# Two transformer blocks on one core: the first mixture slot's rows and weights loaded beside the last attention cells, the tile search cut into steps, one norm moved ahead

## The chip, the core and the metric

The kernel runs on one core of a Trainium2 chip. The core has a matrix engine (PE, with its weight loads shown as PEld), a vector engine (DVE), a scalar engine (ACT), a general engine (POOL), and a queue engine (SP) that issues most transfers. Each engine works through its own list of instructions in order and waits on semaphores where it needs another's result. The metric is the device time of one launch in microseconds.

## The reference

The input `x` is two batches of 1024 tokens of width 256. Two blocks follow each other. All arithmetic is in float32.

- Block 0: self attention with 16 heads of width 16, cross attention to a context of 64 rows, and a mixture of experts: every token is normed, a router picks the 2 best of 8 experts, and the token gets the gated sum of two feed-forward results (256 to 1024, gelu, back to 256), added to `x`.
- Block 1: self attention, cross attention with a mask on the context, and one dense feed-forward of the same size. Each step is preceded by a layer norm and added to `x`.

```
x = latents + mha(ln(latents));  x = x + mha(ln(x), ln(tokens))
logits = ln(x) @ rw.T;  vals, idx = top_k(logits, 2);  gates = softmax(vals)
x = x + sum_k gates[k] * (gelu(ln(x) @ fc1[idx_k].T) @ fc2[idx_k].T)
```

## The kernel before

**Cells and tasks.** Self attention of a block is cut into 128 cells, each with the scores of one head for 128 keys and 512 queries. `self_attention` walks over the cells and, between them, lets a `Stream` of tasks emit other work: projections, cross attention, routing. A task is a Python generator. A positive yield is the cost of what it has emitted; a yield of zero or below asks for a pause before its next step. While cells run, any such pause lasts at least one cell (2.9 us in the planner's count). After the last cell, `Stream.rest` emits what is left: it always takes the able task of the highest rank, and keeps a planner's clock that tells it when a paused task may go on. The order that comes out is fixed when the kernel is built: an instruction that stands behind another on its engine waits for it, whatever the planner thought.

**Units.** The tokens are handled in four units of 512 (0 to 3). For each unit, after its self attention: `project` adds the attention result to `x_sb` (L426 products, L434 addition); `cross_tasks` adds three tasks, a norm (`cnorm`), `weigh` (scores, softmax weights, product) and `share`; `dispatch_task` norms the unit again, routes it (L1268 router product, L1278 to L1357 the choice of two experts and the places) and scatters its rows to `sorted_rows` in memory with eight indirect transfers from POOL (L1365). Then `Mixture.find` works out, from counts so far, which expert each tile of 256 sorted rows belongs to (`expert_tiles` L1378 to L1391, `Places.make` L1413 to L1468, a chain of small DVE instructions) and `Mixture.rows` allows the loads of those rows.

**Slots.** A slot is one tile of 256 rows of one expert. `load_rows` fetches its rows (`xs`), `load_weights` its expert's weights in two halves (`w0` of 2056 columns and `w1` of 2304), each by two transfers on SP. The expert's number and the row come from tables in SBUF that SP reads first (L1495). `turn` transposes the rows (L1550 on PE), applies the norm's scale (L365 on ACT) and works out targets and gates (L1556 to L1573, seven small DVE instructions). `first` makes the hidden layer (L1584 on PE, gelu L1590 on ACT), `second` the result (L1614 on PE, L1607 and L1623 on DVE, an indirect store L1629 on POOL). The first slot has what it needs once units 0 and 1 are dispatched; slots 1 to 4 need unit 2, the others unit 3.

In the kernel before, all tiles for slots lie in pools (`slotw`, `epool`) that open only after the last cell, in memory that the attention used. So the first slot's rows and weights start after it. In `rest`, the task of finding (rank 65) and the routing (70) stand above the norm of unit 3's cross attention (40), and the parts of `find` follow each other without a pause there, since its pauses are only made while cells run:

```
            if maxima[0]:
                yield 0.0
```

`maxima[0]` is true while score cells still need their maxima. `weigh` has two forms by the same switch: with cells running, DVE takes maxima and POOL subtracts; after them, DVE does both (L1101, L1102). The order in the second form is a list of steps: `SC` scores of two row groups (L1081), `TU` transposes of them (L1117) and the exponential on ACT (L1121), `PR` the product with the values and the sums (L1130, L1140) with a reciprocal on DVE (L1149), `DI` the division (L1155 on PE, L1162 on DVE).

**Around the change.** The last heads end with `finish`: sums and results are sent to memory (L470, L471), gathered (L475), the inverse of the sums (L486 on DVE) is sent (L487 `turns`), read back spread out (L491 `by_s`) and multiplied in (L497 on DVE); only then can `project` of unit 3 go on PE (L426).

Of the kernel before, what the change touches and what calls it, by code (L numbers as in the profile page):

```python
# [50 lines left out]
P = 128  # L51
# [148 lines left out]
def two_blocks(  # L200
# [814 lines left out]
    def cross_tasks(stream, layer, n, pool, first):  # L1015


        att = 2 * layer + 1
        w = weights[att]
        b, t0 = n // 2, 4 * n  # L1020
        name = f"c{layer}{n}"
        held = {}

        def norm():
            xT = held["xT"] = pool.tile([P, 2, 512], F32, tag="cx", name=f"xT_{name}")
            yield from norm_task(t0, 4, "cq" if layer == 0 else "ln1", xT, name)
            if layer == 0:
                add_bias(t0, 4, bias_out[1])

        before = [(m, n - 1) for m in ("cross", "weighed")] if n > 0 else ["context"]  # L1030
        stream.add(norm(), 2.0, mark=("cnorm", n), after=before[1:], first=first,
            rank=40)
        stream.add(
            weigh(layer, b, pool, w, name, held), 17.0,
            mark=("weighed", n), after=[("cnorm", n), before[0]], rank=30,
        )
        stream.add(
            share(w, name, t0, held), 5.0, mark=("cross", n),
            after=[("weighed", n)], rank=50,
        )  # L1040

    def weigh(layer, b, pool, w, name, held):
# [148 lines left out]
        for step, *args, wait in (  # L1191
            (SC, 0, 0, None),
            (SC, 0, 1, -1.0),
            (TU, 0, 0, None),
            (SC, 1, 0, None),
            (TU, 0, 1, None),
            (SC, 1, 1, None),
            (PR, 0, None),
            (TU, 1, 0, None),
            (DI, 0, None),  # L1200
            (TU, 1, 1, -1.6),
            (PR, 1, None),
        ):
            step(*args)
            yield {SC: cost, TU: 1.15, PR: 1.1, DI: 0.55}[step]
            if wait:
                yield wait
# [190 lines left out]
    class Places:  # L1398
# [3 lines left out]
        def make(self, pool, name, n, had, caps, last):  # L1402
# [14 lines left out]
            nc.vector.tensor_copy(end[:, E:], caps[-1])  # L1417
            if maxima[0]:
                yield 0.0
            upto = pool.tile([P, 2 * E], F32, tag="ntu", name=f"ntu_{name}", bufs=1)  # L1420
# [9 lines left out]
            self.who = const.tile([P, n], F32, name=f"who_{name}")  # L1430
            if maxima[0]:
                yield 0.0
            row = pool.tile([P, n], F32, tag="row", name=f"row_{name}", bufs=1)
# [5 lines left out]
            nc.vector.tensor_copy(self.at[:, 0, :], row)  # L1439
            if maxima[0]:  # L1440
                yield 0.0

            nc.vector.tensor_tensor(over, over, end.unsqueeze(1).to_broadcast(shape), ALU.mult)
            nc.vector.tensor_reduce(row, over, AX.X, ALU.add)
            nc.vector.tensor_tensor(row, number, row, ALU.subtract)
            if maxima[0]:
                yield 0.0
            nc.vector.tensor_scalar(row, row, begin[:, 0:1], 256.0, ALU.add, ALU.mult)
# [3 lines left out]
            nc.vector.tensor_copy(self.at[:, 1, :], row)  # L1452
            if maxima[0]:
                yield 0.0
            if last:
# [14 lines left out]
    class Mixture:  # L1470
# [3 lines left out]
        def __init__(self, slotw, epool):  # L1474
# [3 lines left out]
            self.caps = []  # L1478


            self.w, self.done, self.ready = ({}, {}), [0, 0], (set(), set())
# [21 lines left out]
        def load_rows(self, s):  # L1503
            xs = self.epool[0].tile([P, 2, WIDE], F32, tag="xs", name=f"xs_{s}", bufs=3)
            row = self.number(s, 1, NROWS - 256)
            nc.sync.dma_start(
                out=xs, in_=sorted_rows[bass.ds(row, 256), :].rearrange("(c p) n -> p c n", p=P)
            )
            self.xs[s] = xs

        def load_weights(self, s, half):
            n = NFF - W_2 if half else W_2
            w = self.w[half][s] = self.slotw[0].tile([P, n], F32, tag=f"w{half}", name=f"w{half}_slot{s}")
            e = self.number(s, 0, E - 1)
# [5 lines left out]
        def load(self, most=NSLOT):  # L1520


            if not self.slotw:
                return
            while len(self.xs) < min(self.nrows, self.turned + 3, self.end):
# [3 lines left out]
            for s in range(min(known, most)):  # L1529
                for half in range(2):  # L1530
                    if s == len(self.w[half]) and s < self.done[half] + 2:
                        self.load_weights(s, half)
# [107 lines left out]
        def find(self, units):  # L1640
# [8 lines left out]
            else:  # L1649

                caps = [self.caps[last], *expert_tiles(f"{units}", (ANY if last else FULL,))]
            if maxima[0]:
                yield 0.0
            pool = self.epool[1] if self.epool else const
# [125 lines left out]
    def block(layer, tail, heads=None, beside=None):  # L1780
# [48 lines left out]
        def when_ready(b, qh, stream, cell):  # L1829
            n = 2 * b + qh  # L1830
            cross_tasks(stream, layer, n, pools["cpool"], cell + 1)
            if layer == 0:
# [7 lines left out]
                if n == 1:  # L1840
                    stream.add(
                        mixture.find(2), 0.3, mark=("found", 2), after=[("counted", 1)], rank=65
                    )
            elif n < 2:
                stream.add(
# [25 lines left out]
    for n in range(2):  # L1871
        epool.append(
            slots.enter_context(tc.tile_pool(name=f"epool{n}", bufs=2 - n, side="right"))
        )
    for units in range(2, 5):
        if units > 2:
# [3 lines left out]
            )  # L1880
        stream.add(
            mixture.rows(units), 0.0, mark=("rows", units), rank=75,
            after=[("found", units), ("dispatch", units - 1)],
        )
    for s in range(NFULL[-1]):
# [181 lines left out]
```

## Time and profile before

| | us |
|---|---|
| median of 3 runs (lowest, highest) | 1640.39 (1638.42, 1646.78) |
| the profiled execution | 1651.84 |
| its span, first to last instruction | 1650.1 |
| PE busy | 1591.0 (96%) |
| DVE, ACT, POOL busy | 981.7, 911.6, 415.2 |
| mean granted PE clock | 0.974 |

The page of the profile gives busy times, the span in 40 slices, and the chain of work that ended last. The trace behind it can be asked for stretches of time, for waits, and for single instructions; the times below are microseconds from the start of the span. A float32 matmul is recorded as two instructions, so a count of 16 in the trace is 8 matmuls in the code.

### The profile page before, as it was taken

Reading aid. Unit: us, or ns where it says so; the run is one execution under the profiler, and the core shown is the slowest. Engines: PE = TensorE matmul, PEld = TensorE weight load, DVE = VectorE, ACT = ScalarE, POOL = GpSimd, SP = SyncE. Lnnn points to the kernel's source line nnn. Section 1 sums busy time; section 2 is a strip of 40 time slices with the busy share of each in tenths; the row PEclk is TensorE's granted clock in tenths of the full one; section 3 lists DMA queues with packets and bytes.
Section 4 is the critical chain, followed back from the end, with each engine's and each line's share of the span. In section 5 each row is a group of like instructions: output and inputs, shape, how many; then the busy total and the mean of one; then the engine's idle time right before and its main releaser. Section 6 shows DMA issues by size and latency. Waiting matters only on the chain.

```text
span 1650.1 us, 28271 instructions
## 1 busy us (share of the span) xinstructions
PE 1591.0 (96%) x10682; PEld 878.9 (53%) x10682; DVE 981.7 (59%) x2092; ACT 911.6 (55%) x1768; POOL 415.2 (25%) x549
## 2 busy tenths in 40 slices
PE   7999999999999977999999999999999999999998
PEld 3433344444443435778888763344444435546766
DVE  5687857688678636431113466876767777845400
ACT  2277867667666853324322327876776676673321
POOL 2134324234335202040112122411322323321000
PEclk7799999999999988999999999999999999999999
DMA  4333510110000024256556421000110002000000
GB/s 141 123 130 113 183 31 21 28 33 31 30 21 34 27 81 167 87 202 237 189 188 236 145 65 34 21 27 14 40 37 23 21 14 82 15 14 21 14 13 26
DMA packets 56591, 122.09 MB, mean 74 GB/s; under 512 B 12546, under 2 KB 26756, under 8 KB 56068
## 3 DMA queue, kind: packets, MB, share of 16 engines
q1 hardware_dynamic: 52612, 110.08, 20.6%
q0 software_dynamic: 3456, 9.51, 1.6%
q8 instruction: 86, 1.41, 0.4%
q10 hardware_dynamic: 384, 0.66, 0.2%
q14 instruction: 53, 0.43, 0.1%
HBM read 72.14 MB, written 39.42 MB: 68 GB/s over the span
## 4 chain that ended last, share of the span: by engine, by line
PE 88%; DVE 7%; DMA 2%; issue 2%; ACT 1%; another core or an unknown queue 0%; POOL 0%; SPq 0%; DVEq 0%; POOLq 0%; ACTq 0%
PE banks L758 16%; PE banks L747 15%; PE banks L809 14%; PE banks L1584 8%; PE banks L1614 8%; PE banks L624 4%; PE banks L1757 3%; PE banks L426 3%; PE banks L1745 3%; DVE mx_s L754 2%; PE banks L594 2%; PE banks L1051 2%; PE banks L1117 2%; PE banks L1081 2%; PE banks L358 1%
## 5 line engine op out<-in xcount | busy, mean ns | idle before, releaser
L754 DVE TENSOR_REDUCE mx_s<-banks 128x1 f32<-128x512 f32 x1024 | 634.5, 683 | 208.9 <-PE banks L747 205.0
L764 ACT ACTIVATE pt_s<-banks 128x512 f32<-128x512 f32 x1024 | 531.2, 607 | 149.6 <-PE banks L747 125.6
L747 PE MATMUL banks<-KS,QS 16*128 16x512 f32 x2048 | 537.2, 638 | 4.2 <-issue 1.9
L758 PE MATMUL banks<-qb_s,KS 32*128 32x512 f32 x2048 | 506.8, 617 | 8.0 <-DVE qb_s L704 4.2
L822 POOL TENSOR_TENSOR acc_s<-acc_s,part_s 128x512 f32<-128x512 f32 x143 | 181.9, 1272 | 429.3 <-ACT part_s L821 417.1
L758 PEld LDWEIGHTS banks<-qb_s,KS 32*128 32x128 f32 x2048 | 176.2, 184 | 179.9 <-DVE mx_s L754 105.4
L809 PE MATMUL banks<-pt_s,v_s 128*20 128x512 f32 x2048 | 262.3, 605 | 0.3 <-ACT pt_s L764 0.2
L747 PEld LDWEIGHTS banks<-KS,QS 16*128 16x128 f32 x2048 | 199.2, 188 | 77.8 <-issue 36.0
L1590 ACT ACTIVATE h_s<-banks,w_slot 128x256 f32<-128x256 f32 x160 | 67.1, 471 | 175.9 <-issue 88.8
L1614 PE MATMUL banks<-w_slot,h_s 128*128 128x256 f32 x640 | 145.0, 383 | 2.8 <-ACT h_s L1590 2.8
L1584 PE MATMUL banks<-xsT,w_slot 128*128 128x256 f32 x640 | 147.0, 382 | 0.7 <-ACT xsT L365 0.7
L809 PEld LDWEIGHTS banks<-pt_s,v_s 128*20 128x20 f32 x2048 | 42.8, 98 | 181.3 <-ACT pt_s L764 128.8
L1614 PEld LDWEIGHTS banks<-w_slot,h_s 128*128 128x128 f32 x640 | 121.8, 192 | 23.5 <-ACT h_s L1590 3.2
L1584 PEld LDWEIGHTS banks<-xsT,w_slot 128*128 128x128 f32 x640 | 119.7, 191 | 20.8 <-DVE mx_s L754 2.3
L821 ACT COPY part_s<-banks 128x512 f32<-128x512 f32 x157 | 93.8, 597 | 63.9 <-PE banks L809 54.8
L1623 DVE SCALAR_TENSOR_TENSOR ys<-banks,gate,b 128x256 f32<-128x256 f32 x40 | 19.3, 483 | 170.3 <-PE banks L1614 166.6
L1629 POOL DMA_INDIRECT results<-ys,to x40 | 38.8, 970 | 268.1 <-DVE ys L1623 224.4
L624 PE MATMUL banks<-xT_s,w_att 128*128 128x512 f32 x128 | 68.1, 667 | 0.0
L1748 ACT ACTIVATE h_f<-banks,w_ff 128x512 f32<-128x512 f32 x32 | 22.0, 688 | 75.0 <-PE banks L1745 75.0
L1102 POOL TENSOR_TENSOR sc_c<-sc_c,mx_c 128x512 f32<-128x512 f32 x38 | 39.6, 1044 | 77.9 <-DVE mx_c L1101 77.9
L1757 PE MATMUL banks<-w_ff,h_f 128*128 128x256 f32 x256 | 57.3, 380 | 0.0
L1745 PE MATMUL banks<-hT_f,w_ff 128*128 128x512 f32 x128 | 56.3, 593 | 0.0
(257 smaller groups left out, 1503.4 us busy)
## 6 DMA issues: line engine op xcount, KB each, us to landing
w_slot<-in_ff_w_dram SPq DMA_DIRECT2D x40, 576.0 KB
w_slot<-in_ff_w_dram SPq DMA_DIRECT2D x40, 514.0 KB
sorted_rows<-fill SPq DMA_DIRECT2D x36, 520.0 KB
whole<-acc_s SPq DMA_DIRECT2D x32, 256.0 KB
xs<-sorted_rows SPq DMA_DIRECT2D x20, 260.0 KB
ot_s<-whole SPq DMA_DIRECT2D x16, 256.0 KB
by_s<-turns SPq DMA_DIRECT2D x16, 256.0 KB
y<-results SPq DMA_DIRECT2D x16, 256.0 KB
```

The source lines that it names most:

```text
L624: nc.tensor.matmul(p, lhsT=w[:, at + k * D + pair * P : at + k * D + (pair + 1) * P], rhs=xT[b][:, k, blk * 512 : (blk + 1) * 512], start= ...
L747: nc.tensor.matmul(sc, lhsT=QS[h % 4][r, qc * P : (qc + 1) * P], rhs=K[r, kh * 512 : (kh + 1) * 512], start=True, stop=True,)
L754: return i, lambda: nc.vector.tensor_reduce(mx[h][:, qc, j, kh : kh + 1], sc, AX.X, ALU.max)
L758: nc.tensor.matmul(sc, lhsT=K[r, n * P : (n + 1) * P], rhs=QB[h][r, :], start=True, stop=True)
L764: nc.scalar.activation(pt, sc, AF.Exp, scale=SCALE)
L809: nc.tensor.matmul(o[32 * j : 32 * j + VW, :], lhsT=V[b][:, cell % 8, 4 * g + j, :], rhs=exps.pop((cell, j)), start=(cell == cells[0]), st ...
L821: nc.scalar.copy(part, o)
L822: helper().tensor_tensor(acc[h], acc[h], part, ALU.add)
L1584: nc.tensor.matmul(ph[:, n, :], lhsT=w[:, at : at + P], rhs=xT[:, k, :], start=(k == 0), stop=(k == 1),)
L1614: nc.tensor.matmul(py, lhsT=h1[:, f, h * P : (h + 1) * P], rhs=w[:, f * D : (f + 1) * D], start=(f == 0), stop=(f == 7),)
L1745: nc.tensor.matmul(ph, lhsT=w1[:, at : at + P], rhs=hT[:, k, :], start=(k == 0), stop=(k == 1))
L1757: nc.tensor.matmul(py[:, n, :], lhsT=h1[:, f, t * P : (t + 1) * P], rhs=w2[:, f * D : (f + 1) * D], start=(f == 0), stop=(f == 7),)
```

## The change

- Slot 0's rows get a tile of their own (`xs_0`) and every third slot's first half of the weights another (`spare`), both in the pool that exists from the start. `load` brings slot 0's two while cells still run, as soon as unit 1 is dispatched and searched; the task `rows` of unit 2 moves into the block for that. The first half of the weights may now be three slots ahead, not two.
- `load` is called once more when the pools open, which emits the second half of slot 0's weights there.
- All pauses in `find` and `make` become `-0.9` and are always made.
- The norm of a unit's cross attention gets rank 67 in block 0, above the search (65).
- In the second form of `weigh`, `PR 0` comes before `SC 1 1`, and `TU 0 1` gets a pause of 1.3.

```diff
-            rank=40)
+            rank=67 if layer == 0 else 40)
...
-            (TU, 0, 1, None),
+            (TU, 0, 1, -1.3),
+            (PR, 0, None),
             (SC, 1, 1, None),
-            (PR, 0, None),
...
-            if maxima[0]:
-                yield 0.0
+            yield -0.9
...
+            self.spare = const.tile([P, W_2], F32, name="spare")
...
-            xs = self.epool[0].tile([P, 2, WIDE], F32, tag="xs", name=f"xs_{s}", bufs=3)
+            if s == 0:
+                xs = const.tile([P, 2, WIDE], F32, name="xs_0")
+            else:
+                xs = self.epool[0].tile([P, 2, WIDE], F32, tag="xs", name=f"xs_{s}", bufs=3)
...
-            w = self.w[half][s] = self.slotw[0].tile([P, n], F32, tag=f"w{half}", name=f"w{half}_slot{s}")
+            if half == 0 and s % 3 == 0:
+                w = self.spare
+            else:
+                w = self.slotw[0].tile([P, n], F32, tag=f"w{half}", name=f"w{half}_slot{s}")
+            self.w[half][s] = w
...
             if not self.slotw:
+                if self.nrows and not self.xs:
+                    self.load_rows(0)
+                    self.load_weights(0, 0)
                 return
...
-                    if s == len(self.w[half]) and s < self.done[half] + 2:
+                    if s == len(self.w[half]) and s < self.done[half] + 3 - half:
...
                         mixture.find(2), 0.3, mark=("found", 2), after=[("counted", 1)], rank=65
                     )
+                    stream.add(
+                        mixture.rows(2), 0.0, mark=("rows", 2), rank=75,
+                        after=[("found", 2), ("dispatch", 1)],
+                    )
...
+    mixture.load()
     for units in range(2, 5):
         if units > 2:
...
-        stream.add(
-            mixture.rows(units), 0.0, mark=("rows", units), rank=75,
-            after=[("found", units), ("dispatch", units - 1)],
-        )
+            stream.add(
+                mixture.rows(units), 0.0, mark=("rows", units), rank=75,
+                after=[("found", units), ("dispatch", units - 1)],
+            )
```

The pause in the third piece of the diff stands six times in the change, five of them in `Places.make` and one in `Mixture.find`. As built, the changed kernel has the same number of instructions on every engine; only their order differs. On PE, after the last attention product, the old order is: transposes of the routing norm (8), transposes of slot 0 (4), router product (2), transposes of the logits (4), `first` of slot 0 (8), projection (8, with the two counting products L1328, L1329 between), `first` (8), counting L1378, `second` (16). The new order is: transposes of slot 0 (4), of the routing norm (8), `first` (4), router product (2), `first` (4), transposes of the logits (4), `first` (8), projection (8, with the same two between), counting, `second` (16). On DVE, the norm of unit 3 now stands in front of most of `find`, whose rest is spread between the norm's last steps. On SP, slot 0's rows and first half stand ahead of head 14's send, its second half ahead of head 15's send, and nothing stands between head 15's gather and its `turns`.

## The prediction

> **What bounds the kernel now.** First the page. PE is busy nearly all the time, and two parts of it hold most of the rest.
>
> ```profile
> PE 1591.0 (96%) x10682; PEld 878.9 (53%) x10682; DVE 981.7 (59%) x2092; ACT 911.6 (55%) x1768; POOL 415.2 (25%) x549
> PEclk7799999999999988999999999999999999999999
> PE 88%; DVE 7%; DMA 2%; issue 2%; ACT 1%; another core or an unknown queue 0%; POOL 0%; SPq 0%; DVEq 0%; POOLq 0%; ACTq 0%
> ```
>
> The chain that ended last is PE for 88%: time is won only where PE stands idle or runs at a lowered clock. The start (first two digits of the clock row) isn't touched. The second dip, near 620 us, is where the change works. The waits of PE from 560 to 760 us:
>
> ```profile
> PE banks L358 <- DVE xd_m L1255: 5.9, 1, 5.9
> PE banks L358 <- DVE xn_c L346: 5.3, 2, 4.1
> PE banks L1550 <- DMA xs<-sorted_rows: 3.0, 1, 3.0
> PE banks L1155 <- DVE inv_c L1149: 2.9, 1, 2.9
> PE banks L1614 <- ACT h_s L1590: 2.8, 1, 2.8
> PE banks L1117 <- DVE sc_c L1102: 1.6, 3, 0.8
> ```
>
> Columns: total us, times, longest. The first three are the routing norm of unit 2, the norm of unit 3 and slot 0's rows. Then stretches of the clock (PE busy is the second number, the granted clock the third from the right):
>
> ```profile
> 597.70:601.10 3.40, 0.00 (x0) 0.00 (x0) 2.70 (x16) 0.00 (x0) 0.00 (x0) 1.00 0.21 80
> 601.10:604.50 3.40, 1.97 (x8) 1.54 (x8) 1.64 (x5) 1.72 (x4) 0.00 (x0) 0.50 0.66 174
> 607.90:611.30 3.40, 3.27 (x4) 0.27 (x2) 0.00 (x0) 0.96 (x3) 0.00 (x0) 0.50 0.81 315
> 631.80:635.20 3.40, 0.81 (x4) 0.38 (x2) 1.65 (x10) 0.00 (x0) 1.36 (x2) 1.00 0.94 301
> 642.00:645.40 3.40, 3.40 (x6) 1.34 (x5) 0.00 (x0) 0.69 (x1) 0.00 (x0) 0.50 1.01 401
> 659.10:662.50 3.40, 0.74 (x6) 0.75 (x7) 2.57 (x4) 0.49 (x1) 0.00 (x0) 1.00 0.00 0
> 662.50:665.90 3.40, 3.40 (x15) 3.18 (x14) 0.69 (x1) 1.52 (x3) 0.00 (x0) 0.50 0.00 0
> ```
>
> After a stretch with little work the clock is half; it returns only after a full one. So idle costs twice: the router product, from the PE timeline, at half and at full clock:
>
> ```profile
> 607.59 3.58 PE L1268 MATMUL banks<-hT_m,rw 128*8 128x512 f32 x4
> 689.95 1.88 PE L1268 MATMUL banks<-hT_m,rw 128*8 128x512 f32 x4
> ```
>
> Last the queue. SP issues slot 0's weights ahead of the inverse sums, whose transfer then takes 7.8 us:
>
> ```profile
> 602.56 2.26 SPq L1518 DMA_DIRECT2D w_slot<-in_ff_w_dram  x4
> 604.92 0.55 SPq L487 DMA_DIRECT2D turns<-sums_s  x1
> 612.75 0.69 SPq L491 DMA_DIRECT2D by_s<-turns  x1
> ```
>
> At the head pair before (550.94) the same `turns` needed 1.5 us, and `by_s` after it 3.6.
>
> **Part 1: rows and weights early.** The table for unit 2 is ready at 551.2 and unit 1's last scatter is issued at 532.0, so SP can issue the early loads between 553 and the next send at 570.4; the 1.3 MB land long before 595.7, where the last attention product ends. No transfer waits behind them until 570.4, and PE is covered by cells there: cost nothing. If SP were held to 580, head 14's send has until 597.
>
> From 595.7 on PE, old: idle to 601.62 (5.9), transposes 1.97, idle 3.0, slot 0's transposes, router product 3.58, and so on; counting L1378 starts at 625.32. New, with durations of the trace:
> - Slot 0's transposes at 595.7 (0.60 at full clock). The wait for `xd_m` stays: the DVE list up to L1255 is unchanged (601.16). Idle 5.3 instead of 5.9, so the clock still falls.
> - 601.6: transposes 2.0 at half clock; from here PE has work without a break. The return of the clock needs a full stretch of 3.4, begun at an unknown phase: between 605.0 and 608.4, I take 606.7. `first` (4 matmuls, 1.86 full) crosses it: to 607.0. Router product 1.88: 608.9. `first` 1.86 hides the ACT step lT (0.68, old wait 0.77): 610.7. Logits 0.4: 611.1. `first` 3.6: 614.7.
> - Projection needs `by_s`. Slot 0's second half (1.18 MB) now waits on SP for the last L809 (595.7), stands ahead of head 15's send, and takes 3.5 us at 340 GB/s (rows of 601 to 611). That send is issued at 597.1 as before but lands about 602 (before 599.8). L486 now stands behind seven small DVE instructions: 604.2. `turns` 604.3, lands 606.2; `by_s` 609.8. L497 follows L1281 at 611.4 and ends 612.1: no wait before 614.7, 2.6 us to spare. If that cover went, each us late delays projection and routing by one.
> - The routing choice on DVE (612.1, some 13 instructions of 0.22) gives `chosen` at 614.8, needed at 616.5. Projection 3.6 and counting products 0.7: 619.0; L1378 ends 619.2 against 625.6. **PE is 6.2 us ahead.**
>
> **Part 2: norm before search.** `second` of slot 0 (7.15) ends at 626.4. Second L434 ends at 619.8 (before 622.76). Behind it stood 3.3 of statistics and places, 5.1 of search (26 instructions, 625.89 to 631.0), 4.35 of the root chain, b 0.6, ys. Now: statistics 3.3, three search instructions 0.6, b 0.6, root chain 2.9 to 4.4 (14 of 0.2; old stalls 1.5 may stay), five search 0.8, ys 0.4, four search 0.8: first `xn_c` at 629.2 to 630.6, transposes 0.4 later, 629.6 to 631.0 against 636.67: 5.7 to 7.1 ahead. The PE wait stays 3 to 4.6 (was 4.1). The second pair comes 2.9 behind the first (eight search instructions and a ys between), before 2.4: minus 0.5. What the moved search delays: slot 1's weights issue at 631 to 632.4 (before 629.65), its rows two transfers later at about 635.5 (before 638.88, behind twice the weights), landed about 641. PE's slot 1 and 2 transposes ask for them about 642, in front of the cross attention's transposes.
>
> **The clock there.** The Trainium skill, "TensorE: Matmul & The Clock Gate", Part 1, lets the clock fall after a window of 3.4 us that was idle. Taken strictly, a pause of about 3.9 holds a whole idle window rarely (0.5 of 3.4), and L1051 would run 4 matmuls in about 3.8 (twice L1268's 1.88) instead of 5.99: 2.2 more gained, 3.4 with the transposes. But here the clock fell after 659.1 to 662.5, which was 22% busy with a pause of only 2.85. I go by the row: half clock again, L1051 5.99, nothing gained. Ahead after L1051: **6.0** (5.2 to 6.6).
>
> **Part 3: order in `weigh`.** Counting from L1081's start (646.73 old): DVE takes 1.33 per row group. Old: six groups, 14 turn instructions 2.2, two groups, then L1149 at 660.75; PE waited 0.8, 0.3, 0.6, 2.85, and then 3.4 us ran at half clock (1.6 lost). L426 ended at 32.05. New, from TU 0 1 (ends 7.3): four `first` 1.9, PR 0 1.9, SC 1 1 1.1, TU 1 0 (its scores ready at 11.4) to 13.5; L1149 already at 11.4 to 12.35, so DI 0 13.5 to 14.5 without wait; TU 1 1 to 15.8 (last group 15.0); `first` 17.7, PR 1 19.6, `first` 23.3, DI 1 24.3, then L426 directly behind DI 1 waits for L1162 (0.85): ends 28.8. **3.3 ahead**, with no pause long enough to lower the clock. ACT loads two more tables (1.28 each, as L1121's row) at 8.5 and 11.3, both before its next input. `second` of slot 1 (7.07) and four `first` (1.9) then cover the routing norm of unit 3: DVE needs 8.1 of their 9.0.
>
> In block 1's tail the same list saves the wait on L1149 (0.8 of 1440 to 1651); SC 1 1 later may give half back: 0.4. The third buffer for first halves: PE has no wait on weights in 680 to 1010, worth nothing, and the same bytes move.
>
> **Sum.** 6.0 + 3.3 + 0.4 = 9.7 us: the profiled execution from 1651.84 to about 1642. It lies 11.5 above the median, and none of these steps is known to shrink without the profiler: 1640.39 - 9.7 = 1630.7.
>
> **Rivals.**
> - More (0.16): the clock does not fall at the norm of unit 3, or rises sooner in part 1, and PE's stall of 2.8 at 713.8 on a gelu goes with the shift. 3.4 + 1.5 more and perhaps 2.8: gain 13 to 18, 1622 to 1627.
> - Partly (0.29): DVE stalls (0.6, 0.9 at 633, beside POOL's scatter) grow as the search's small instructions sit between the norm's, and `by_s` or rows 1 and 2 come 2 to 4 late. Gain 3 to 8: 1632 to 1638. The row for it: DMA share 1.0 from 638.6 to 645.4.
> - Slower (0.05): slot 1 and 2's transposes stand before TU 0 0 in PE's list; rows queue behind 2.2 MB of weights and the scatter. If the second lands later than 642, all of cross attention waits one for one; it decides beyond about 652, and at 655 the kernel is 3 us slower, 1643. Against it: the old rows, issued at 638.88 behind 4.5 MB, were there by 648.4.
>
> The likeliest (0.50) is the sum, 8.2 to 13: 1627 to 1632. 0.5% is 8.2 us, about what a measurement of this kernel can tell from no change. So faster 0.50 + 0.16 = 0.66, same 0.29 (within 8.2), slower by more 0.05 at most, counted whole. Range 1621 to 1638: the likeliest, nearly all of More and most of Partly.
>
> **What would show it.** In the changed profile: L1550 of slot 0 before the routing transposes with no wait on `xs`; router product near 1.9 to 2.5; `turns` to `by_s` 2 us apart; L1378 about 6 us earlier; `xn_c` wait still 3 to 5; no wait of L1155 on `inv_c` near 655; L426 after it 9 ahead, and the gap kept to the end. Wrong if L426 of unit 3 waits on `ot_s`, if L1550 of slot 1 waits on DMA, or if slots later wait for weights.

## The result and the profile after

The changed kernel took 1630.71 us (median of 6 runs, 1625.98 to 1635.94) where the kernel before took 1643.72 in the same comparison (6 runs, 1638.42 to 1647.64): ratio 0.9923, 95% interval 0.9895 to 0.9951, a gain of 12.7 us with 8 to 17 inside the interval. A second measurement of the same kernel beside other runs of before gave 0.9931 (0.9907 to 0.9955). The forecast was 9.7 us. That the median lies within 0.1 us of the forecast time of 1630.7 is luck: the median of before in this comparison is 3.3 us above the 1640.39 from which the forecast subtracted, and the gain is 3.0 us above the forecast one.

Three rows of the page after, to be held against those of before: busy time of PE, the clock row, and the chain.

```profile
PE 1581.6 (97%) x10682; PEld 871.1 (53%) x10682; DVE 982.0 (60%) x2092; ACT 912.3 (56%) x1768; POOL 415.0 (25%) x549
PEclk8899999999997998999999999999999999999999
PE 91%; DVE 6%; issue 1%; DMA 1%; ACT 1%; POOL 0%; SPq 0%; DVEq 0%; POOLq 0%; ACTq 0%
```

PE does the same 10682 instructions and stays the engine that bounds the kernel. Of the 20.9 us by which this profile's span is shorter, 9.4 are busy time of PE (the same work, less of it at half clock) and 11.5 are its idle time. The waits of PE from 560 to 760 us say which waits went:

```profile
PE banks L358 <- DVE xn_c L346: 5.7, 3, 2.6
PE banks L358 <- DVE xd_m L1255: 5.4, 1, 5.4
PE banks L1117 <- DVE sc_c L1102: 1.7, 3, 0.8
PE banks L1592 <- ACT xsT L365: 0.7, 1, 0.7
PE banks L1051 <- ACT xT_c L365: 0.7, 1, 0.7
PE banks L426 <- DVE q_c L1162: 0.4, 1, 0.4
PE banks L1329 <- DVE before_m L1321: 0.3, 1, 0.3
```

Gone are the waits for `xs` (3.0), for `inv_c` (2.9), for `ot_s` (1.2), for `lT_m` (0.8) and for a gelu `h_s` (2.8; this last one turns out not to be the change's, see the repeat below). The waits for `xd_m` (5.4, before 5.9) and `xn_c` (5.7 in three pieces, before 5.3 in two) remain, as the prediction had them. The PE timeline of the changed stage (start, length, what runs; in brackets the idle time before it). Lines behind the diff have moved by 8: L1550 is now L1558, L1584 is L1592, L1614 is L1622.

```profile
595.77 0.66 PE L1558 MATMUL banks<-ident,xs 128*128 128x128 f32 x4
601.79 1.97 PE L358 MATMUL banks<-ident,xd_m 128*128 128x128 f32 x8 [5.36 <-DVE xd_m L1255]
603.55 3.04 PE L1592 MATMUL banks<-xsT,spare 128*128 128x256 f32 x8
606.51 1.88 PE L1268 MATMUL banks<-hT_m,rw 128*8 128x512 f32 x4
...
618.05 0.28 PE L1378 MATMUL banks<-inside,ones 128*128 128x8 f32 x2
618.19 7.15 PE L1622 MATMUL banks<-w_slot,h_s 128*128 128x256 f32 x32
627.96 0.76 PE L358 MATMUL banks<-ident,xn_c 128*128 128x128 f32 x4 [2.61 <-DVE xn_c L346]
630.55 0.69 PE L358 MATMUL banks<-ident,xn_c 128*128 128x128 f32 x2 [1.84 <-DVE xn_c L346]
632.45 0.69 PE L358 MATMUL banks<-ident,xn_c 128*128 128x128 f32 x2 [1.21 <-DVE xn_c L346]
633.79 6.76 PE L1051 MATMUL banks<-xT_c,w_att 128*128 128x512 f32 x8 [0.66 <-ACT xT_c L365]
640.48 1.72 PE L1081 MATMUL banks<-kbd,q_c 32*128 32x128 f32 x32
642.14 1.09 PE L1558 MATMUL banks<-ident,xs 128*128 128x128 f32 x8
...
653.39 1.06 PE L1155 MATMUL banks<-inv_c,picks 128*128 128x128 f32 x8
...
665.14 3.29 PE L426 MATMUL banks<-w_att,q_c 128*128 128x256 f32 x14 [0.42 <-DVE q_c L1162]
```

Slot 0's transposes stand right behind the last attention product, the router product runs at 1.88 (3.58 before), L1155 at 653.39 has no wait, and slot 1's transposes at 642.14 find their rows.

To compare kernels whose profiles start a few us apart, the times below are counted from the start of the last L809 product of block 0 (592.46 before, 592.60 after). The lead of a kernel at a landmark is how much sooner than in before it is reached from there:

| lead over before, us | L1378 starts | L1081 starts | last `q_c` L426 of unit 3 ends | end of the span |
|---|---|---|---|---|
| after | 7.4 | 6.4 | 10.5 | 21.0 |
| the same kernel, again | 6.8 | 7.1 | 11.2 | 11.9 |

The change acts up to the third column and is worth about 11 us there in both profiles. The first pair of profiles differs by another 10.5 us behind it, the second by 0.7. So those 10.5 are not the change: in the first profile after, one stall of 2.8 us was missing, and behind the third column the clock did not fall again within the span, where before has five windows of 3.41 us at half clock (at 717, 980, 1471 and 1488).

### The profile page after: what moved, and what is told of

It reads as the page before. It is cut to its first block, busy times and chain, and to the rows that moved or that the text cites. A ratio compares the mean times of both kernels' runs of the same rounds, so it can differ in the third digit from the quotient of the medians.

```text
span 1629.2 us, 28274 instructions
## 1 busy us (share of the span) xinstructions
PE 1581.6 (97%) x10682; PEld 871.1 (53%) x10682; DVE 982.0 (60%) x2092; ACT 912.3 (56%) x1768; POOL 415.0 (25%) x549
## 3 DMA queue, kind: packets, MB, share of 16 engines
q1 hardware_dynamic: 52612, 110.08, 20.9%
## 4 chain that ended last, share of the span: by engine, by line
PE 91%; DVE 6%; issue 1%; DMA 1%; ACT 1%; POOL 0%; SPq 0%; DVEq 0%; POOLq 0%; ACTq 0%
PE banks L758 17%; PE banks L747 15%; PE banks L809 14%; PE banks L1592 8%; PE banks L1622 8%; PE banks L624 4%; PE banks L1764 3%; PE banks L1752 3%; PE banks L426 3%; PE banks L1051 2%; PE banks L594 2%; PE banks L1081 2%; PE banks L1117 2%; DVE mx_s L754 2%; PE banks L358 1%
## 5 line engine op out<-in xcount | busy, mean ns | idle before, releaser
L809 PE MATMUL banks<-pt_s,v_s 128*20 128x512 f32 x2048 | 262.3, 605 | 0.7 <-DVE sc_c L1102 0.5
L1622 PE MATMUL banks<-w_slot,h_s 128*128 128x256 f32 x640 | 143.1, 380 | 0.0
L809 PEld LDWEIGHTS banks<-pt_s,v_s 128*20 128x20 f32 x2048 | 42.5, 98 | 181.2 <-ACT pt_s L764 128.9
L1622 PEld LDWEIGHTS banks<-w_slot,h_s 128*128 128x128 f32 x640 | 120.7, 190 | 19.8 <-DVE mx_s L754 1.5
L1598 ACT ACTIVATE h_s<-banks,w_slot 128x256 f32<-128x256 f32 x104 | 43.7, 471 | 119.3 <-issue 65.7
L1592 PE MATMUL banks<-xsT,w_slot 128*128 128x256 f32 x416 | 95.7, 381 | 0.7 <-ACT xsT L365 0.7
L1592 PEld LDWEIGHTS banks<-xsT,w_slot 128*128 128x128 f32 x416 | 77.3, 190 | 14.8 <-DVE mx_s L754 2.3
```

The costliest lines, as they stand in the source:

```text
L809: nc.tensor.matmul(o[32 * j : 32 * j + VW, :], lhsT=V[b][:, cell % 8, 4 * g + j, :], rhs=exps.pop((cell, j)), start=(cell == cells[0]), st ...
L1592: nc.tensor.matmul(ph[:, n, :], lhsT=w[:, at : at + P], rhs=xT[:, k, :], start=(k == 0), stop=(k == 1),)
L1622: nc.tensor.matmul(py, lhsT=h1[:, f, h * P : (h + 1) * P], rhs=w[:, f * D : (f + 1) * D], start=(f == 0), stop=(f == 7),)
```

## The experiments

All kernels were timed beside runs of before; the gain in us is one minus the ratio times the median of before in that comparison (1647.97, 1649.11 or 1649.53). Leads are from one profile each.

| kernel | ratio to before (95%) | gain, us | lead at L1378 | at L1081 | end of L426 |
|---|---|---|---|---|---|
| first part alone | 0.9987 (0.9971 to 1.0003) | 2.1 | 7.9 | 3.9 | 5.6 |
| second part alone | 0.9993 (0.9978 to 1.0007) | 1.2 | 0.9 | 3.4 | 3.5 |
| third part alone | 0.9969 (0.9954 to 0.9985) | 5.1 | 1.0 | 1.8 | 5.9 |
| whole change, again | 0.9931 (0.9907 to 0.9955) | 11.4 | 6.8 | 7.1 | 11.2 |
| without the third part | 0.9960 (0.9941 to 0.9979) | 6.6 | 7.4 | 6.4 | 8.1 |
| without the second part | 0.9941 (0.9921 to 0.9960) | 9.7 | 6.8 | 3.9 | 8.0 |
| search in one piece | 0.9954 (0.9937 to 0.9970) | 7.6 | 7.0 | 4.2 | 8.3 |
| weights two ahead | 0.9938 (0.9919 to 0.9957) | 10.2 | 6.5 | 6.7 | 10.8 |
| few fillers | 0.9929 (0.9908 to 0.9951) | 11.7 | 6.6 | 4.6 | 8.7 |
| more fillers | 0.9917 (0.9896 to 0.9938) | 13.7 | 9.0 | 7.2 | 11.3 |
| both `xn_c` pairs first | 0.9949 (0.9924 to 0.9974) | 8.4 | 6.8 | 13.7 | 8.6 |
| the same with fillers | 0.9949 (0.9934 to 0.9964) | 8.4 | 8.6 | 15.5 | 10.3 |

The lead at the end of L426 and the timed gain agree within about 3.5 us everywhere, so the profile can be read stage by stage. Gains of single rows carry some 2.5 to 4 us either way. A lead has scatter too: the second and the third part alone are built like before up to L1378 and still lead by 0.9 and 1.0 there, because slot 0's rows happened to keep PE waiting for 2.1 and 2.3 us and not 3.0.

**The first part alone.** Against before it holds all of the change but the rank, the pauses of the search and the list in `weigh`:

```diff
+                xs = const.tile([P, 2, WIDE], F32, name="xs_0")
...
+                w = self.spare
...
+                    self.load_rows(0)
+                    self.load_weights(0, 0)
```

> Only the first part of the change: slot 0's rows and first weights in places of their own, asked for beside the last cells, and slot 3's first weights after them; the search, the norm's rank and the weigh order stay as before. Theory (the parts act one by one, along TensorE's order): the wait of the transposes for xs (3.0 us before) is gone, L1378 ends near 618.3 as with the whole change, some 7 us ahead of before; the norm is still put behind the search, so TensorE waits for xn_c longer than before (7 us and more in place of about 4), and L1051 starts only 1 to 3 us ahead of before; inv_c still holds L426 by about 2.9 us. Lead at the end of unit 3's last L426: 1 to 3 us, time 1 to 4 us below before. Rival 1 (the early weights are the whole change): the lead of 7 us lasts to L426, and the time is that of the whole change, 10 us or more below. Rival 2 (rows and weights were hidden anyway, another wait takes their place): L1378 ends at 624 or later, no lead.

Two rows of its PE waits from 560 to 760 us:

```profile
PE banks L358 <- DVE xn_c L346: 8.6, 2, 7.3
PE banks L1155 <- DVE inv_c L1149: 2.9, 1, 2.9
```

L1378 is 7.9 us ahead as foretold, and by L1081 half of that is given back: the longest wait for `xn_c` is 7.3 in place of 4.1, because DVE still does the whole search first. `inv_c` still holds PE. The lead at L426 of 5.6 was above the 1 to 3 expected; 1.7 of it is phase of the clock: with the same wait for `inv_c`, before ran on at half clock and this kernel did not (from L1081 to the end of L426 32.05 and 30.36 us). The rest of the surplus was there at L1051 already, which starts 4.6 us ahead and not 1 to 3. The timed gain, 2.1, cannot be told from nothing. "The early weights are the whole change" falls, and so does "hidden anyway" for the stage up to L1378.

**The second part alone.**

```diff
-            rank=40)
+            rank=67 if layer == 0 else 40)
...
-            if maxima[0]:
-                yield 0.0
+            yield -0.9
```

> Only the second part: the norm of unit 3 at rank 67 and the search in steps; rows, weights and the weigh order as before. Theory: up to L1378 nothing is won (the wait for xs of 3.0 us stays, L1378 ends at 625 to 626); then xn_c is ready sooner than before against L1378: before its first transposes ran 11 us after L1378, with the change 9.7 us after it; L1051 starts 1 to 3 us ahead of before, and the time is 1 to 3 us below before. Rival (the search is put off by the norm, and the rows of slot 1 with it): the wait moves to slot 1's transposes after L1081, 2 us or more, and the lead at L1081 is zero or below.

L1051 starts 2.6 us ahead, of which 0.9 are the scatter at L1378, and the gain is 1.2 (-1.2 to 3.6): what was expected, and too small to be measured by itself. The rival, slot 1's transposes waiting for their rows, did not show: the only wait for `xs` from 560 to 760 us is the one of slot 0.

**The third part alone.**

```diff
-            (TU, 0, 1, None),
-            (SC, 1, 1, None),
+            (TU, 0, 1, -1.3),
             (PR, 0, None),
+            (SC, 1, 1, None),
```

> Only the third part: the order of transposes, scores and picks in the first units' memory attention. Theory: nothing changes up to L1081; from the start of L1081 to the end of unit 3's last L426 it takes 28 to 29 us in place of 32.05, since L426 no longer stands behind inv_c (2.9 us before); time 3 to 4 us below before. It acts in units 0 to 2 as well where they have the same form. Rival 1: the gain needs the rows of slot 1 early (first part), and alone it is below 1 us. Rival 2: scores put back by the transposes make VectorE late, and the wait for sc_c grows by as much as inv_c gives back.

From the start of L1081 to the end of L426 it took 27.97 us in place of 32.05; the wait for `inv_c` is gone and those for `sc_c` stay at 1.6. It is the only part whose gain alone can be told from nothing: 5.1 us (2.5 to 7.6), with the 4.1 between these landmarks inside the interval.

**The whole change again, and without one part.** The undone parts are the diffs above, taken back.

> The whole change, once more, beside the kernels with one part undone. Theory: 11 to 14 us below before (12.7 +- 4.6 so far); from the start of the last L809 of block 0 to the end of unit 3's last L426 75 to 76.5 us, where before took 86.3. If half of the 20.9 us between the first two profiles was phase of the clock and one stall (L1590 6.31 us late at 716 in before), the two profiles of this pair differ by another sum, but by some 10 us up to L426 again. Rival (the 10 us after L426 belong to the change): again 20 us between the profiles, the stall missing and the clock full at the same places.

> The whole change without the weigh order of its third part. Theory: as up to L1081 with the whole change (lead of 6 to 7 us over before), then 31 to 32 us from L1081 to the end of L426 in place of 28, with the wait for inv_c of 2.8 us back; time 3 to 5 us above the whole change, 8 to 9 below before. Rival (the order alone is worth 5 us only because rows are late without the first part): less than 2 us above the whole change.

> The whole change without its second part: norm of unit 3 back at its old rank and the search unstepped; early rows and weights and the weigh order stay. Theory: L1378 as with the whole change (7 us ahead of before), then TensorE waits 7 us and more for xn_c, as it did with the first part alone (7.3), and the lead at L1081 is 4 us in place of 6.3; time 2 to 4 us above the whole change. Rival (the norm's rank does nothing, since alone it gave 1.1 +- 2.4 us): within 1 us of the whole change, and the wait for xn_c no longer than its 5.7 us.

The repeat gave a lead of 11.2 us at L426 and only 11.9 at the end, so the rival (20 us are the change's) falls. Its PE waits show the stall of the first profile before again:

```profile
PE banks L1622 <- ACT h_s L1598: 2.8, 1, 2.8
```

Without the third part L1081 to L426 takes 30.36 us and L1155 waits 2.85 for `inv_c`; with it 27.95. So the list is worth 2.4 us when the clock does not fall behind the wait, and 4.1 when it does, as in before. Timed, the kernel without it is 4.8 above the whole change, with intervals that overlap (3.5 to 9.7 and 7.4 to 15.3). Without the second part the wait for `xn_c` is 7.3 and the lead at L1081 3.9 in place of 6.4 to 7.1; timed, 1.7 above, inside the scatter. The three parts alone lead by 15.0 us in sum, together by 11. That is no loss in working together: 0.9 of the second part's lead stood at L1378 and 1.8 of the third's at L1081, where these kernels are still built like before, and 1.7 of the first's is the clock behind `inv_c`. Without these the parts sum to 10.6. Timed, they sum to 8.4 against 11.4, which the intervals don't tell apart.

**The search in one piece, with the norm's new rank.**

```diff
-            yield -0.9
+            if maxima[0]:
+                yield 0.0
```

> The whole change with the search in one piece as before; the norm's rank of 67 stays. Theory: the rank alone puts the norm's statistics and roots before the search, as without steps the search comes in one or two pieces after them: xn_c's wait 4 to 7 us, rows of slot 1 at most 2 us later or earlier than with steps; lead at L426 9.5 to 12 us, time within 2 us of the whole change. Rival (steps are what lets xn_c out): the search of 5 us stands whole before xn_c, wait of 7 us and more as with the second part undone, lead 8 us.

```profile
PE banks L358 <- DVE xn_c L346: 8.6, 2, 7.3
PE banks L1563 <- DMA xs<-sorted_rows: 0.6, 1, 0.6
```

The rival holds: 7.3 us and a lead of 8.3, the same as with the whole second part undone (7.3 and 8.0). DVE's order from the statistics to the second pair is the same in both kernels, so the rank without pauses moved nothing. Pauses without the rank were not run: whether the pauses need the rank is open.

**First weights two slots ahead.**

```diff
-                    if s == len(self.w[half]) and s < self.done[half] + 3 - half:
+                    if s == len(self.w[half]) and s < self.done[half] + 2:
```

> The whole change with first weights asked for two slots ahead as before, not three (the places stay). Theory: no wait on weights in either kernel, the third place is worth nothing: landmarks as with the whole change within 0.7 us, time within 2 us of it, weights of slot 1 and its rows sent at the same times or a little earlier. Rival 1 (three ahead does harm: its 0.5 MB stand before rows): L1558 of slot 1 earlier and the lead at L426 larger. Rival 2 (it does good later): a wait of TensorE on weights appears in 690 to 960, the lead falls after L426.

Lead 10.8 against 10.5 and 11.2: the third place's lead is worth nothing here, as predicted.

**Fillers against the clock.** A few transposes of `ident` into a bank nobody reads, in the waits:

```diff
+    def warm(n):
+        i, wp = bank()
+        for k in range(n):
+            nc.tensor.transpose(wp[:, (k % 4) * P : (k % 4 + 1) * P], ident, ident)
+        free.append(i)
...
             xT, to, gate = self.turn(s)
+            if s == 0:
+                warm(12)
...
                 if h == 1:
                     self.did(s, 1)
+                    if s == 0:
+                        warm(8)
...
             affine(dst[:, :, t0 * P : (t0 + 2) * P], i, tp, ln)
+            if tag == "c03" and t0 == 0:
+                warm(6)
```

> The whole change, with transposes of the identity into a bank nobody reads, as fillers in two waits: 12 after slot 0's rows are turned (where TensorE waits 5.4 us for xd_m), 8 after slot 0's second product and 6 after the first pair of the norm (waits for xn_c, 5.7 us in three). They add no wait of their own if they are shorter than the wait. Theory (the clock falls behind these waits, and that is what L1592 at 3.0 and L1051 at 6.76 us pay): granted clock stays full from 600 to 645, L1592 takes 1.9 to 2.1 us in place of 3.04 and 1.99 at once, L1051 3.8 to 4.5 in place of 6.76, lead of 3 to 5 us over the whole change at L1081, time 3 to 5 us below it. Rival 1 (the fillers take their time from the path): xd_m's transposes start up to 2 us later, and nothing or less than nothing is won. Rival 2 (the cost was not the clock but the operands arriving late): the durations stay at 3.04 and 6.76.

They ran in 1.47, 1.04 and 0.82 us at the start of each wait, and the clock fell all the same: what was left of the waits was still long. L1060 (L1051 of the other kernels) took 6.74. The lead at L1081 even fell to 4.6, since L1060 waited 1.60 us for `xT_c` (0.66 in the repeat): the rival that fillers cost time on the path is right in part. Whether a full clock would pay was not tested by this run, and it was tried again with 36, 20, and 14 and 6:

> The whole change with more of the fillers: 36 transposes of the identity after slot 0's rows (some 4.4 us at 0.12 each), 20 after slot 0's second product, 14 and 6 after the two pairs of the norm. With 12, 8 and 6 the clock still fell, after windows of 3.41 us in which TensorE was busy 10% and 42%. Theory (the clock falls where such a window is under some 45% busy): no half clock from 595 to 650 of the profile, L1601 (first product) 8 matmuls in 1.9 to 2.1 us and L1060 in 3.6 to 4.2 in place of 6.74; 3 to 5 us below the whole change unless the fillers hold back what follows them. Rival 1: the fillers hold the path by what they are longer than the wait (up to 2 us each), and the sum is nothing. Rival 2: the clock falls for another reason than idle TensorE, half clock stays, and the time is that of the whole change.

The PE timeline of this kernel; L365 is the filler, L1601, L1277 and L1060 are L1592, L1268 and L1051 of the profile after.

```profile
598.75 4.09 PE L365 MATMUL banks<-ident 128*128 128x128 f32 x36
604.26 1.41 PE L358 MATMUL banks<-ident,xd_m 128*128 128x128 f32 x8 [1.42 <-DVE xd_m L1264]
605.51 1.89 PE L1601 MATMUL banks<-xsT,spare 128*128 128x256 f32 x8
607.33 1.89 PE L1277 MATMUL banks<-hT_m,rw 128*8 128x512 f32 x4
...
636.66 5.58 PE L1060 MATMUL banks<-xT_c,w_att 128*128 128x512 f32 x8 [1.08 <-ACT xT_c L372]
```

At the first wait the theory holds: with 4.09 us of the 5.4 filled, the clock stayed, `first` ran in 1.89 instead of 3.04 to 3.62, and L1378 is 9.0 us ahead, about 2 more than without. At the second it did not: PE was busy 1.64 of the 3.41 us from 630.53, and the clock fell. The 2 us were lost again between the transposes of `xn_c` and L1060, and the lead at L1081 is 7.2, as in the repeat. DVE is not the cause: its second pair ends 38.3 us from the start of L809, in the repeat 40.4, and PE's transposes of it keep this lead. It was ACT that began late, first in this kernel, then in the repeat:

```profile
635.13 1.93 ACT L372 ACTIVATE xT_c<-banks,cols 128x256 f32<-128x256 f32 x4 [17.13 <-PE banks L358]
```

```profile
634.33 1.02 ACT L365 ACTIVATE xT_c<-banks,cols 128x256 f32<-128x256 f32 x2 [11.68 <-issue]
638.75 1.02 ACT L365 ACTIVATE xT_c<-banks,cols 128x256 f32<-128x256 f32 x2 [3.40 <-PE banks L358]
```

(The line of this step is L372 with fillers, L365 without.) In the repeat ACT takes each pair within 0.1 us of the recorded end of PE's transposes (634.29 and 638.72). With fillers behind the pairs it begins both at 635.13, though the first pair's transposes are recorded as done at 629.68 and the second's at 633.92: PE's signal came late. Why is not known. The time is 2.3 us below the repeat of the whole change, with intervals that overlap widely: not shown to be better.

**Both `xn_c` pairs ahead of the search.** In the profile after, DVE puts search steps between the inverse roots and the first pair, and more before the second. Here are DVE and POOL of that profile:

```profile
627.49 0.73 DVE L346 TENSOR_SCALAR xn_c<-x_sb,mv_c,rs_c 128x256 f32<-128x256 f32 x2
...
630.10 2.30 DVE L346 TENSOR_SCALAR xn_c<-x_sb,mv_c,rs_c 128x256 f32<-128x256 f32 x2
...
632.83 1.90 DVE L1448 CAST at<-row 128x4 int32<-128x4 f32 x1
```

```profile
630.96 1.27 POOL L418 TENSOR_TENSOR x_sb<-x_sb,bias_out 128x512 f32<-128x512 f32 x1
...
633.41 1.27 POOL L418 TENSOR_TENSOR x_sb<-x_sb,bias_out 128x512 f32<-128x512 f32 x1
```

The second pair and a cast of four numbers per row end within 0.2 us of the two additions on POOL (632.23 and 634.68). So an edit that takes both pairs at once:

```diff
         inverse_roots(rs[:, :nt], mv[:, :nt, 1], tag, pool, engine or helper())
+        if then is not None:
+            then((mv, rs))
...
+        def early(at):
+            for t0 in range(0, nt, 2):
+                both[t0] = center(src, (t0, t0 + 1), at, tag, pool)
```

> The whole change, and in the norm of unit 3 both pairs of L346 (xn_c) are put directly behind the inverse roots, ahead of the search's steps. With the change, VectorE ran nine small steps of the search and ys before the first pair (1.5 us) and nine more and ys before the second, which then took 2.30 us in place of 0.73 while GpSimd's add L418 (630.96 to 632.23) ran. Theory (VectorE's order there is what TensorE waits for): first pair 1.5 us and second some 5 us earlier, wait for xn_c 2 us or less in place of 5.7, L1051 starts 3 to 4 us earlier; then slot 1's rows, which come no earlier, hold L1558 by 1 to 4 us, so that 0 to 3 us of it are left at the end of L426. Rival 1 (the rows take all of it): the lead at the end of L426 is 11 us as before, or less. Rival 2 (the search is what VectorE owes next): rows later by 1.5 us, and the lead falls below 10.

> As the kernel before it in this row (both xn_c pairs behind the inverse roots), with 36 filler transposes behind slot 0's rows, which alone kept the clock full at 600 and brought L1378 2.1 us forward, all of it given back to xn_c. Theory: what the fillers bring is no longer given back at xn_c, L1378 some 9 us ahead of before, L1051 11 to 13 us ahead; whatever the rows of slot 1 allow reaches the end, 12 to 15 us ahead of before at L426. Rival: rows of slot 1 are the bound from there, and both kernels of this row end alike.

The PE timeline of the first of the two:

```profile
631.78 1.43 PE L360 MATMUL banks<-ident,xn_c 128*128 128x128 f32 x8 [1.23 <-DVE root_c L322]
634.10 3.70 PE L1061 MATMUL banks<-xT_c,w_att 128*128 128x512 f32 x8 [0.89 <-ACT xT_c L367]
637.73 1.85 PE L1091 MATMUL banks<-kbd,q_c 32*128 32x128 f32 x32
648.01 1.97 PE L1568 MATMUL banks<-ident,xs 128*128 128x128 f32 x8 [8.43 <-DMA xs<-sorted_rows]
649.78 1.91 PE L1127 MATMUL banks<-ident,sc_c 128*128 128x128 f32 x8
```

The wait for `xn_c` is down to 1.2 us, the clock stays, the projection L1061 takes 3.70 instead of 6.76, and at L1081 the kernel is 13.7 us ahead of before. Then PE stands 8.4 us for slot 1's rows: it asks for them 7.2 us sooner than after the change (counted from L809), and they are there 1.3 us or more later. PE runs on at half clock (1.91 for the eight transposes that take 1.1 at full), and leads by only 8.6 at L426. Rival 2 (the rows come later, the lead falls below 10) was right, and by a way that was not expected. DVE and POOL of this kernel:

```profile
634.53 2.85 DVE L1443 TENSOR_SCALAR row<-who 128x4 f32<-128x4 f32 x1
...
634.85 2.50 POOL L428 TENSOR_TENSOR x_sb<-x_sb,bias_out 128x512 f32<-128x512 f32 x2
```

A step of the search that takes 0.17 elsewhere lasted 2.85, until both additions of POOL were over. The requests for rows, in this kernel and then in the profile after:

```profile
641.59 2.15 SPq L1516 DMA_DIRECT2D xs<-sorted_rows  x3
```

```profile
635.32 2.15 SPq L1506 DMA_DIRECT2D xs<-sorted_rows  x3
```

From the start of the last L809 product (597.20 here) that is 44.4 us, and 42.7 after the change. The second kernel, with 36 fillers in the first wait, repeats all of it 1.8 us sooner (lead 15.5, wait 8.5, lead 10.3): what these fillers win at the first wait reaches L426, where no fillers stand behind `xn_c`. Timed, the two kernels gain the same 8.4, and neither beats the change.

## Why the prediction was right

**Part 1** foretold PE 6.2 us ahead at L1378; two profiles gave 7.4 and 6.8. Its steps: slot 0's transposes at 595.7 (595.77); idle of 5.3 before `xd_m` (5.36); half clock until 606.7 (605.9, the router product at 1.88); `turns` at 604.3 (604.07) and `by_s` issued behind it about 2 us later (606.05); L497 without stall; end of L1378 at 619.2 (618.3). (The text's own ends, 619.2 against 625.6, make 6.4; it says 6.2.) The sum let 6.0 of them pass L1051 because part 2 brings `xn_c` forward too; the first part alone, which keeps 3.9 of 7.9, shows that this condition holds.

**Part 2** foretold 6.0 after L1051, from first transposes at 629.6 to 631.0 and L1051 at half clock. Measured 6.4 and 7.1; the first transposes ran at 627.96, ahead of the range, since DVE's chain of inverse roots had no stall. The second pair was taken as 2.9 behind the first. Its second half came 4.5 behind, as DVE was held by POOL's addition: a term that was too small. The choice at the clock, the row rather than the strict rule, was right: L1051 took 6.76 in one profile and 5.41 in the other, and not 3.8; but 3.70 when the pause was only 1.2. What the text called "norm before search" it did not split: the rank without the pauses does nothing.

**Part 3** foretold 3.3; L1081 to L426 shrank by 4.1 in both profiles (32.05 to 27.95). L426's wait for `q_c` is 0.4 where 0.85 was taken. Taken out of the whole change it costs only 2.4, since the other 1.7 was the lowered clock in before, which depends on where the wait falls.

**The rest.** The tail of block 1 was given 0.4. From the first L1081 of its last unit to the end it took 117.9 us before, 117.6 in the profile after (0.3 gained) and 119.2 in the repeat, where the clock fell in it: not shown to be worth anything. The third place was given nothing and shows no worth. The sum of 9.7 against 12.7 and 11.4 timed: short by the 1 to 2 us that the parts gave more at L426 (10.5 and 11.2 where 9.3 was foretold), and by scatter.

**The rivals.** More (13 to 18) is what the first pair of profiles seems to show, 20.9 us with the gelu stall gone. But the clock did fall at the norm of unit 3, and the repeat, which has that stall and gains 11.9 between profiles, says that the rest was no part of the change. The timed intervals (8 to 17, 7 to 15) don't rule that rival out by themselves. Partly names the right weakness (the search's steps between those of the norm, beside POOL), but it cost about 1.6 us, and the gain stayed above that rival's 3 to 8. Slower named slot 1's rows as what could hold all of cross attention. After the change the margin is thin: rows in time at 642.14, a wait of 0.6 with the search in one piece. In the kernels with both pairs first PE came to these rows 7 us sooner than after the change and paid it all back in waiting: the path that this rival named is the next bound.

## What to carry to other kernels

An early start on one engine's list is worth only what the next shared input allows: find the next wait in the list (rows, then norm, then rows again) before adding up gains, and undo parts one at a time. Count a part's lead from the point up to which its kernel is built like before: here the parts alone seem to sum to 15 us where the whole gives 11, and 4.4 of that was scatter and phase of the clock. A higher rank in a planner moves nothing if the other task has no pause in which it can be passed over. Take two profiles of a kernel before explaining a difference behind the stage that was changed: 10 of 21 us in the first pair were not there in the second.

## What the runs showed of the hardware

**The clock's windows.** Counted over the 14 profiles from 100 us on, in a grid of 3.41 us laid at the clock's own changes, with PE's busy share in each window: all 40 windows at full clock with less than 40% were followed by half clock; of 198 windows between 40% and 80%, 30 were; of 5891 above it, 16 were. All 86 returns to full clock followed a window of 80% or more, but 43 other windows of 80% or more at half clock were not followed by a return. So a wait of 2.6 to 2.9 us can lower the clock or not, by where it falls in the grid: before's wait for `inv_c` did, the same wait in the kernel with the first part alone did not. The Trainium skill ("TensorE: Matmul & The Clock Gate", Part 1) asks for an idle window; here one with 40% of work was not enough to keep the clock, and even 48% failed in the kernel with more fillers.

**A clock that fell behind a busy PE.** 13 of the 16 falls behind busy windows follow one in which PE was busy all the time, as here in the repeat, where the next window ran at half clock:

```profile
1523.49:1526.90 3.41, 3.41 (x63) 1.00 0.02 5
```

These windows hold little but products of 1 and of 32 rows by 128 columns (L1072 and L1081). Counted in the same way, all 13 windows of which such products fill 84% to 98% were followed by half clock, and with PE busy throughout, none was of the 2 that they fill to 76% and 81%, nor of the 91 between 60% and 74%. So the recorded busy share is not all that the clock goes by, and small products may count for less; no run was made to test it.

**DVE waits for POOL.** A pair of L346 took 0.73 us alone and 2.30 across POOL's addition of 1.27; a step of 0.17 took 2.85 across two. Each of these ends within 0.2 us of POOL's end and begins 0.3 to 0.9 us before the addition's recorded start. The Trainium skill ("SBUF: two separate sides" in "SBUF — State Buffer") describes a port pair that VectorE, in a mode with two ports or with two inputs in SBUF, and GpSimd hold by turns for a whole instruction, the other being blocked. The rows agree with it; which mode DVE's instructions ran in, no row shows.

**A stall left open.** In 13 of 14 profiles ACT's third pair of gelus of one slot comes after 6.3 us of idle time (at 716.09 in before), though PE's product for it is recorded as done 6 us sooner, and PE's signals then come seven within 0.4 us. It costs PE 2.8 us and is missing only in the first profile after. What causes it was not found, nor whether the late signal behind the fillers is the same thing.
